# A selective-scan kernel on one core: loads of B, evacuation of the sums and the multiply of carried states placed later in the slot order

## The chip, the cores and the metric

The kernel runs on one core of a Trainium2 chip. The core has a tensor engine (PE, with PEld for its weight loads), a vector engine (DVE), a scalar engine (ACT), a general engine (POOL) and a sync engine (SP), each with its own instruction queue, and 16 DMA engines between HBM and on-chip memory. The metric is the device time of one execution in microseconds (us), median of several runs.

## The reference

The input is `x` of shape (8, 96, 128, 128), float32. Layer 0 adds to `x` a convolutional LSTM over the rows of a group-normalised `x`. Layer 1 adds to that a wavelet block: a wavelet transform of the group-normalised input, an attention factor on the three high bands, and on the low band (64 x 64 positions, so L = 4096) layer norm, a projection, a 3 x 3 convolution and a selective scan in four directions with 192 channels and 16 states. Then come a norm, a gate, a projection and the inverse wavelet transform. The scan is the part that the change touches:

```python
xs = jnp.concatenate([x_hwwh, jnp.flip(x_hwwh, -1)], axis=1)      # rows, columns, both reversed
x_dbl = jnp.einsum('bkdl,kcd->bkcl', xs, x_proj_w)
dts, Bs, Cs = jnp.split(x_dbl, [DT_RANK, DT_RANK + D_STATE], axis=2)
delta = jax.nn.softplus(...)                                       # from dts
def step(hst, inp):
    u_t, d_t, B_t, C_t = inp
    dA = jnp.exp(d_t[..., None] * A)
    hst = dA * hst + (d_t * u_t)[..., None] * B_t[:, :, None, :]
    y = jnp.einsum('bkdn,bkn->bkd', hst, C_t)
    return (hst, y)
_, ys = jax.lax.scan(step, h0, seq)
```

## The kernel before, in words

Layer 0 fills the first 3000 us or so. Then comes one long loop, `for s in range(total)` (L1140), of 3072 slots. A slot scans two states (GN = 2) over 512 positions (CH = 512) for 128 lanes, each lane a channel of one of two directions. Four slots (PASS = 4) are a pass over half of the states. A chunk of 512 positions takes 24 slots: two halves of the states, r = 0 and 1, and in each half three groups of lanes, q = 0, 1, 2. An image has 8 chunks in forward order (p = 0) and 8 in reverse (p = 1), and there are 8 images, so 128 chunks. `place(s)` (L908) gives chunk, r, q, the number of the block of B and C, and the first state. Slot numbers below are within the chunk, 0 to 23; a number over 23 is a slot of the next chunk.

What a slot does, engine by engine:

- ACT: `decay(s + 1)` (L1006) makes two exponentials, 128 x 512 each, into a PSUM tile `da`, of which there are two. At L1152 it copies the last column of the slot before as the carried state.
- POOL: `product(s + 3)` (L994) multiplies `du` by a tile `bt` of B for the slot three ahead (L1001), and adds the carried states to the border column (L1004).
- DVE: `scan(s)` (L1021) runs the recurrence at L1025, then in three slots of four L1191 multiplies by a tile `ct` of C. In the first slot of a pass (`by_pool`, L1014) POOL does that multiply one slot later (L1199).
- PE: `add_up` (L1027) transposes and adds the result into one PSUM tile `py` for the pass, which has a single buffer.
- SP: `load_bc(k, cols)` (L981) issues the load of block k of B (cols 0) or of C (cols 1), as two DMAs of 256 KB. There are five buffers of each. A block serves the same slot of the passes q = 0, 1 and 2; in the pass q = 2 it is used for the last time, and then block k + 5 goes into its buffer. B is loaded at the end of slot s for the block of slot s + 2 (L1202), and C for the block of slot s - 2 (L1204). So B is loaded in slots 6 to 9 and 18 to 21, C in slots 10 to 13 and 22 to 25. Three of four such blocks are first needed by slots 13, 14, 15 and 25, 26, 27 (the last three are slots 1, 2, 3 of the next chunk); the fourth is needed twelve slots later.

`evacuate` (L1088) runs in the first slot of each pass. ACT copies the finished `py` out of PSUM, into `half` when r = 0 (L1095), into `y` when r = 1 (L1102). For r = 1 it also enters a job: `y_store` (L1052), which stores y from ACT's DMA queue (p = 0), or `y_out` (L1056), which transposes it on PE, copies it on ACT and stores a part from ACT's queue at L1066 (p = 1).

All other work (wavelet analysis, projections, softplus, output, synthesis) is cut into jobs: generators that yield an engine, a cost, a number of half slots to wait since the job's last step, and resources that they take and give. `background` (L1132) is called once in the first slot of a pass and twice in the other three, and `now` counts these calls: they are the half slots. Each call gives every engine a budget (PE 1.1, ACT 0.9, DVE 0.7, POOL 1.3 us) and writes the job steps that fit. `border` (L956) is such a job: ACT makes the factor `ac` of the carried states (L965), then POOL multiplies it by them (L968) and sets a border column of `dl` (L969). `pin` (L453) fixes the order of the instructions on each engine as written.

Two rules of the built program matter too. SP and ACT issue their DMAs in order. All DMAs complete on eight semaphores, handed out in turn, and a DMA is not issued before the previous DMA of its semaphore has landed, whichever queue that one is on.

Of the kernel before, what the change touches and what calls it, by code (L numbers as in the profile page):

```python
# [56 lines left out]
def forward_kernel(ctx: ExitStack, tc: tile.TileContext, i, out):  # L57
# [29 lines left out]
    with ExitStack() as s:  # L87
# [15 lines left out]
        def place(lanes, chunk, src):  # L103
            for m in range(3):
                nc.sync.dma_start(wq[lanes, chunk, m, 0:96], src[:, m, :])
                nc.sync.dma_start(wq[lanes, chunk, m, 96:128], src[:, 3, 32 * m:32 * m + 32])
# [124 lines left out]
    with ExitStack() as s:  # L231
# [143 lines left out]
        for k in range(4):  # L375
            r, p, h0 = dtrow[k], k // 2, k % 2
# [76 lines left out]
        def pin():  # L453
            traced = tc.nc.cur_bb.bb.instructions
            for ins in traced[seen[0]:]:
                prev = pinned.get(ins.engine)
                if prev is not None:
                    tc.add_manual_dep(ins, prev.name, mybir.DependencyInfo(
                        mybir.DependencyClass.NoSync, mybir.DependencyReason.DATA), reason="order of the slots")
                pinned[ins.engine] = ins  # L460
            seen[0] = len(traced)
# [68 lines left out]
        BANK, SHORT, NONE = ("bank",), ("short",), ()  # L530

        def hasten(job):
            if not job.done and job.rank > -1e9:
                job.due, job.rank = min(job.due, now[0]), -1e9
                for a in job.after:
                    hasten(a)

        def drain(until):

            for job in until:  # L540
                hasten(job)
            jobs.sort(key=lambda j: j.rank)
            while not all(j.done for j in until):
                big = dict(SP=1e9, PE=1e9, ACT=1e9, DVE=1e9, POOL=1e9)
                write(dict(big), EARLY)
                write(dict(big), LATE)
                now[0] += 1
                pin()
# [351 lines left out]
        order = [(p, c) for p in range(2) for c in (range(NCHK) if p == 0 else reversed(range(NCHK)))]  # L900
        chunks = [(b, p, c) for b in range(B) for p, c in order]
        PASS = NS // GN // 2
        SLOTS = 6 * PASS
# [10 lines left out]
        def edges(ci):  # L914

            return (0, CH - 1) if chunks[ci][1] == 0 else (CH - 1, 0)

        def is_first(ci):
            return ci % NCHK == 0

        def is_last(ci):
            return ci % NCHK == NCHK - 1
# [33 lines left out]
        def border(ci, q):  # L956


            b, p, c = chunks[ci]
            e0 = edges(ci)[0]  # L960
            yield "ACT", 0.25, 1, NONE, NONE
            dl = inputs[ci, q][0]
            if not is_first(ci):
                ac = inputs[ci, q][2] = sp.tile([128, NS], F32, name="ac", bufs=6)
                nc.scalar.activation(ac, av[:, p, q, :], AF.Exp, scale=dl[:, e0:e0 + 1])  # L965
            yield "POOL", 0.4, 1, NONE, NONE
            if not is_first(ci):
                nc.gpsimd.tensor_mul(ac, ac, carries[b, p][:, q, :])  # L968
            nc.gpsimd.memset(dl[:, e0:e0 + 1], 1e30)  # L969
# [11 lines left out]
        def load_bc(k, cols):  # L981

            if k < NBLOCKS:
                (b, p, c), n0 = chunks[k // (2 * PASS)], GN * (k % (2 * PASS))
                if not all(j.done for j in analysed[b][0]):
                    drain(analysed[b][0])
                t = bcts[k, cols] = bcp.tile([128, GN, CH], F32, name="bt" if cols == 0 else "ct", bufs=5)
                n0 = 2 * n0 + GN * cols
                for h0 in range(2):
                    nc.sync.dma_start(t[64 * h0:64 * h0 + 64],  # L990
                                      bc_d[b][2 * p + h0, n0:n0 + GN, c * CH:c * CH + CH].unsqueeze(0)
                                      .to_broadcast([64, GN, CH]))
# [13 lines left out]
        def decay(s, j):  # L1006
            if s < total:
                ci, r, q, k, n0 = place(s)
                p = chunks[ci][1]
                if j == 0:  # L1010
                    das[s] = psh.tile([128, GN, CH], F32, name="da")
                nc.scalar.activation(das[s][:, j], inputs[ci, q][0], AF.Exp, scale=av[:, p, q, n0 + j:n0 + j + 1])  # L1012

        def by_pool(s):  # L1014
            return s % PASS == 0

        def halves(s):

            return 2 * s - (s + PASS - 1) // PASS
# [30 lines left out]
        stored, back, quarter, turns, flushed, ys = {}, {}, [], [], [], []  # L1050
# [81 lines left out]
        def background(**full):  # L1132

            for eng, us in full.items():
                left[eng] = us + min(left.get(eng, 0), 0)
            write(left, EARLY)
            write(left, LATE)
            now[0] += 1

        for s in range(total):  # L1140
            at_slot[0] = s
            ci, r, q, kb, n0 = place(s)
            b, p, c = chunks[ci]

            if by_pool(s - 3):
                add_up(s - 3)
            if not by_pool(s - 1):
                add_up(s - 1)

            if s and not by_pool(s - 1) and not is_last((s - 1) // SLOTS):  # L1150
                pc, _, pq, _, pn = place(s - 1)
                nc.scalar.copy(carries[chunks[pc][0], chunks[pc][1]][:, pq, pn:pn + GN], das[s - 1][:, :, edges(pc)[1]])  # L1152
            das.pop(s - 1, None)
            for j in range(GN):
                decay(s + 1, j)
            if s and s % PASS == 0:
                evacuate(s - 1)
            slot, step = s % SLOTS, ci % len(order)
            if slot == 0:
                if step == 0:  # L1160


                    if b > 0:
                        outs = output(b - 1, now[0] + 4, now[0] + 0.25 * IMAGE, turns)
                        synthesis(b - 1, now[0] + 0.2 * IMAGE, now[0] + 0.97 * IMAGE, [*outs, analysed[b - 1][1]])
                    turns = []
                    if b + 1 < B:
                        analysed[b + 1] = analysis(b + 1, now[0] + 4, now[0] + 0.71 * IMAGE)
                if is_first(ci):
                    carries[b, p] = sp.tile([128, 3, NS], F32, name="carry")  # L1170
                if ci + 1 < len(chunks):
                    after = analysed[b + 1][0] if step + 1 == len(order) else []
                    now0[0] = now[0] - halves(s)
                    dt_job[ci + 1] = add(now[0], load_dt(ci + 1), after, urgent=1000)
                    for t in range(3):
                        prepare(ci + 1, t, after)
                if p == 1:
                    back[ci] = [add(now[0] + 2 * (8 + PASS * t), forward_sum(ci, b, c, t), after=[stored[b, c, t]],
                                    take=("yf",), urgent=1000)
                                for t in range(3)]  # L1180
            if p == 1 and r == 1 and slot % PASS == 0 and not back[ci][q].done:
                drain([back[ci][q]])
            pool = by_pool(s)
            background(SP=1e9, PE=1.1, ACT=0.9, DVE=0.7, POOL=1.3)
            scan(s)
            product(s + 3)
            xb = xbs.pop(s)
            if not pool:
                background(SP=1e9, PE=1.1, ACT=0.9, DVE=0.7, POOL=1.3)
                hc = sums[s] = sp.tile([128, GN, CH], F32, name="hc")  # L1190
                nc.vector.tensor_mul(hc, das[s], bcts[kb, 1])  # L1191
            else:
                made = s, xb
            if by_pool(s - 1):
                sp1, xb = made
                pc, _, pq, pk, pn = place(sp1)
                if not is_last(pc):
                    nc.gpsimd.tensor_copy(carries[chunks[pc][0], chunks[pc][1]][:, pq, pn:pn + GN], xb[:, :, edges(pc)[1]])
                nc.gpsimd.tensor_mul(xb, xb, bcts[pk, 1])  # L1199
                sums[sp1] = xb  # L1200

            if place(s + 2)[2] == 2:  # L1202
                load_bc(place(s + 2)[3] + 5, 0)
            if s > 1 and place(s - 2)[2] == 2:  # L1204
                load_bc(place(s - 2)[3] + 5, 1)
            if r == 1 and slot % PASS == PASS - 1:
                free["dl"] += 1
            pin()
# [68 lines left out]
```

## Time and profile before

| | us |
|---|---|
| median of three runs | 15879.47 (15873.98 to 15884.72) |
| the profiled execution, its own time | 15881.9 |
| its span, first to last instruction | 15880.1 |
| stretch of the 3072 scans, first start to last end | 3567.9 to 15379.0, 11811.1 |
| busy in that stretch: DVE, POOL, PE, ACT | 10509.8, 10270.6, 8686.6, 7300.1 |
| DMA in that stretch | 0.72 of the 16 engines' time, 162 GB/s |

The page gives busy time by engine, then the span in 40 slices, DMA queues, groups of instructions (`out<-in`, count, busy us, mean ns, idle us of the engine before them and what ended it), and DMA issues. The view of waits gives who waited for whom: us in total, how many times, the longest. For SP a wait is time in which its queue stood still. Line numbers are those of the kernel before.

### The profile page before, as it was taken

How to read it: one execution, taken by the hardware profiler on the slowest of the kernel's cores; microseconds unless marked ns; L12 is line 12 of the kernel's file. 1: busy time of each engine (PE TensorE's matmuls, PEld its weight loads, DVE VectorE, ACT ScalarE, POOL GpSimd, SP SyncE). 2: the span in 40 equal slices, each digit the busy share in tenths (PEclk: the TensorE clock that was granted, in tenths of full speed). 3: DMA queues.
4: the chain of work that ended last, by engine and by line, in shares of the span. 5: the costliest groups of instructions: out<-in, count | busy, mean ns of one | idle time of the engine just before them, and what ended most of it. 6: DMA issues, size and time to landing. Idle time of an engine off the chain costs nothing. (4 is left out here: it accounts for less than half of the span.)

```text
span 15880.1 us, 146749 instructions
## 1 busy us (share of the span) xinstructions
PE 12017.8 (76%) x42850; PEld 6570.4 (41%) x42850; DVE 11728.4 (74%) x8612; ACT 8726.4 (55%) x15473; POOL 11270.4 (71%) x9544
## 2 busy tenths in 40 slices
PE   2999999586776777777777777777777777766666
PEld 0444444234444444444444444444444444444432
DVE  4333333209999988998899889888998898899871
ACT  0444444236766665666566656655665566555440
POOL 1333333009899987997798889878987898799760
PEclk9999999788887988888888888888888898877876
DMA  7333333246767777776777777777777777766653
GB/s 166 72 73 72 71 64 66 55 93 167 166 145 164 173 162 157 172 178 153 158 176 170 156 166 174 167 159 164 176 167 156 165 175 164 154 148 145 143 113 78
DMA packets 2458101, 2239.33 MB, mean 141 GB/s; under 512 B 1322929, under 2 KB 1523058, under 8 KB 2457043
## 3 DMA queue, kind: packets, MB, share of 16 engines
q1 hardware_dynamic: 1313491, 2007.56, 54.7%
q10 hardware_dynamic: 1143808, 222.38, 8.5%
q8 instruction: 344, 5.64, 0.2%
q14 instruction: 458, 3.75, 0.1%
HBM read 1862.20 MB, written 367.03 MB: 140 GB/s over the span
## 5 line engine op out<-in xcount | busy, mean ns | idle before, releaser
L1001 POOL TENSOR_TENSOR xb<-du,bt 128x1024 f32<-128x1024 f32 x3072 | 7245.7, 2362 | 330.9 <-DMA bt<-bc_d 169.6
L1025 DVE TENSOR_TENSOR_SCAN da<-da,xb 128x1024 f32<-128x1024 f32 x2304 | 5262.9, 2284 | 377.2 <-ACT da L1012 356.7
L1012 ACT ACTIVATE da<-dl,av 128x512 f32<-128x512 f32 x6144 | 4249.6, 692 | 1044.7 <-DVE hc L1191 494.7
L1039 PE MATMUL py<-ident,hc 128*128 128x128 f32 x18432 | 2882.3, 308 | 2400.6 <-DVE hc L1191 2272.9
L1039 PEld LDWEIGHTS py<-ident,hc 128*128 128x128 f32 x18432 | 2402.5, 159 | 3526.6 <-issue 1478.3
L1191 DVE TENSOR_TENSOR hc<-da,ct 128x1024 f32<-128x1024 f32 x2304 | 2813.2, 1221 | 552.5 <-DMA ct<-bc_d 390.9
L181 PE MATMUL pg<-hx,wq 128*128 128x512 f32 x4608 | 2019.7, 592 | 0.0
L1199 POOL TENSOR_TENSOR xb<-xb,ct 128x1024 f32<-128x1024 f32 x768 | 1809.3, 2356 | 99.3 <-DVE xb L1025 45.6
L1152 ACT COPY carry<-da 128x2 f32<-128x2 f32 x2016 | 319.9, 159 | 2721.8 <-DVE hc L1191 2492.7
L1025 DVE TENSOR_TENSOR_SCAN xb<-da,xb 128x1024 f32<-128x1024 f32 x768 | 1750.1, 2279 | 60.9 <-ACT da L1012 48.3
L584 PE MATMUL pd<-ph,wa 128*128 128x512 f32 x2304 | 1223.2, 663 | 262.7 <-ACT ph L578 142.3
L811 PE MATMUL pd<-ph,wg 128*128 128x504 f32 (+1 forms) x2304 | 1214.1, 659 | 204.5 <-DMA ph<-ll_d 124.4
L181 PEld LDWEIGHTS pg<-hx,wq 128*128 128x128 f32 x4608 | 871.7, 189 | 1106.7 <-issue 1106.3
L198 POOL TENSOR_TENSOR x1b<-xb,hx 96x512 f32<-96x512 f32 x256 | 302.7, 1183 | 1369.7 <-DVE hx L197 1124.4
L186 ACT ACTIVATE gate<-pg,gbias 32x512 f32<-32x512 f32 x768 | 523.3, 681 | 1185.2 <-PE pg L181 1185.2
L644 PE MATMUL pc<-xp,wc 97*128 97x512 f32 x2304 | 1143.6, 627 | 3.4 <-ACT bcs L674 3.4
L1039 PE MATMUL py<-ident,xb 128*128 128x128 f32 x6144 | 1006.5, 318 | 142.4 <-POOL xb L1199 140.5
L1039 PEld LDWEIGHTS py<-ident,xb 128*128 128x128 f32 x6144 | 879.2, 167 | 543.2 <-issue 266.7
L192 DVE TENSOR_TENSOR gate<-gate,gate 96x512 f32<-96x512 f32 x256 | 186.7, 729 | 840.9 <-ACT gate L186 840.9
L584 PEld LDWEIGHTS pd<-ph,wa 128*128 128x128 f32 x2304 | 452.7, 212 | 745.2 <-issue 439.9
L811 PEld LDWEIGHTS pd<-ph,wg 128*128 128x128 f32 x2304 | 461.7, 215 | 677.5 <-issue 580.3
L178 PE MATMUL pg<-x,wq 128*128 128x512 f32 x1536 | 703.4, 594 | 14.7 <-POOL x L168 14.7
(179 smaller groups left out, 12317.9 us busy)
## 6 DMA issues: line engine op xcount, KB each, us to landing
bt<-bc_d SPq DMA_DIRECT2D x2048, 256.0 KB
ct<-bc_d SPq DMA_DIRECT2D x2048, 256.0 KB
raw<-x_d SPq DMA_DIRECT2D x384, 288.0 KB
xb<-in_x SPq DMA_DIRECT2D x64, 1536.0 KB
du<-u_d SPq DMA_DIRECT2D x768, 128.0 KB
wa<-wa_d SPq DMA_DIRECT2D x192, 384.0 KB
xs<-in_x SPq DMA_DIRECT2D x64, 1024.0 KB
x_d<-x1b SPq DMA_DIRECT2D x792, 64.0 KB
```

Source lines behind the costliest of these rows:

```text
L178: nc.tensor.matmul(pg[m], wq[:, 3, m, :], xk[:, r, bs, 0:W], start=True, stop=False)
L181: nc.tensor.matmul(pg[m], wq[:, tap, m, :], hk[:, r, bs, tap:tap + W], start=False, stop=(tap == 2))
L186: nc.scalar.activation(gg[32 * m:32 * m + 32], pg[m][96:128], AF.Tanh, bias=gbias[96:128, m:m + 1])
L584: nc.tensor.matmul(pd, wa[:, 3 * ty + tx, :], ph[:, ty:ty + 8, tx:tx + W2], start=(ty == tx == 0), stop=(ty == 1 and tx == 2))
L644: nc.tensor.matmul(pc, wc[:, tap, d0:d0 + 128], xp[:, r + ty:r + ty + 8, tx:tx + W2], start=(tap == 0), stop=(tap == 8))
L811: nc.tensor.matmul(pd[:, :, c0:c1], wgs[g][:, 3 * ty + tx, :], ph[:, ty:ty + 8, c0 + tx - 1:c1 + tx - 1], start=(k == 0 and tx == 1), stop ...
L1001: nc.gpsimd.tensor_mul(xb, du.unsqueeze(1).to_broadcast([128, GN, CH]), bcts[k, 0])
L1012: nc.scalar.activation(das[s][:, j], inputs[ci, q][0], AF.Exp, scale=av[:, p, q, n0 + j:n0 + j + 1])
L1025: nc.vector.tensor_tensor_scan(h, da, xb, 0.0, ALU.mult, ALU.add)
L1039: nc.tensor.matmul(pys[key][:, 128 * t:128 * t + 128], hc[:, j, 128 * t:128 * t + 128], ident, is_transpose=True, skip_group_check=True, s ...
L1191: nc.vector.tensor_mul(hc, das[s], bcts[kb, 1])
L1199: nc.gpsimd.tensor_mul(xb, xb, bcts[pk, 1])
```

## The change

Three edits. The job `border` waits two half slots instead of one between ACT's factor and POOL's multiply. The load of B is written one slot later, in slots 7 to 10 and 19 to 22. The first call of `background` in a slot moves ahead of `evacuate`; the block that enters the jobs of the next chunk in slot 0 stays behind `evacuate`, so it too comes after that call. In the first slot of a pass that call is the only one.

```diff
-            yield "POOL", 0.4, 1, NONE, NONE
+            yield "POOL", 0.4, 2, NONE, NONE
...
             for j in range(GN):
                 decay(s + 1, j)
+            slot = s % SLOTS
+            if p == 1 and r == 1 and slot % PASS == 0 and not back[ci][q].done:
+                drain([back[ci][q]])
+            pool = by_pool(s)
+            background(SP=1e9, PE=1.1, ACT=0.9, DVE=0.7, POOL=1.3)
             if s and s % PASS == 0:
                 evacuate(s - 1)
-            slot, step = s % SLOTS, ci % len(order)
+            step = ci % len(order)
             if slot == 0:
...
-            if p == 1 and r == 1 and slot % PASS == 0 and not back[ci][q].done:
-                drain([back[ci][q]])
-            pool = by_pool(s)
-            background(SP=1e9, PE=1.1, ACT=0.9, DVE=0.7, POOL=1.3)
             scan(s)
             product(s + 3)
...
-            if place(s + 2)[2] == 2:
-                load_bc(place(s + 2)[3] + 5, 0)
+            if place(s + 1)[2] == 2:
+                load_bc(place(s + 1)[3] + 5, 0)
```

## The prediction

> **What bounds the kernel now.** I read the page first, then who waited for whom on DVE, SP, POOL and ACT, then the timeline around one long wait. From the page:
>
> ```profile
> PE 12017.8 (76%) x42850; PEld 6570.4 (41%) x42850; DVE 11728.4 (74%) x8612; ACT 8726.4 (55%) x15473; POOL 11270.4 (71%) x9544
> DVE  4333333209999988998899889888998898899871
> ...
> L1025 DVE TENSOR_TENSOR_SCAN da<-da,xb 128x1024 f32<-128x1024 f32 x2304 | 5262.9, 2284 | 377.2 <-ACT da L1012 356.7
> L1191 DVE TENSOR_TENSOR hc<-da,ct 128x1024 f32<-128x1024 f32 x2304 | 2813.2, 1221 | 552.5 <-DMA ct<-bc_d 390.9
> ```
>
> PE has the largest total, but that is an average over stages. The row of digits shows DVE at 8 and 9 tenths from the tenth slice on: in the stretch of the scans (11811.1 us) DVE is busy 10509.8, so it sets the pace, and only its 1301 idle us can be won. The last two lines name the two largest pieces: 390.9 us waiting for a C load, 356.7 for ACT's exponentials. The waits:
>
> ```profile
> DVE hc L1191 <- DMA ct<-bc_d: 390.9, 110, 12.9
> DVE da L1025 <- ACT da L1012: 356.7, 174, 8.8
> ```
>
> ```profile
> SPq L990 <- POOL xb L1004: 1040.7, 436, 17.0
> SPq L990 <- DMA y_d<-y: 283.3, 40, 10.7
> ```
>
> ```profile
> POOL ac L968 <- ACT ac L965: 443.1, 176, 13.5
> POOL xb L1001 <- DMA bt<-bc_d: 169.6, 57, 9.1
> POOL xb L1001 <- DVE da L1025: 133.0, 72, 6.9
> ```
>
> ```profile
> ACT y L1102 <- PE py L1039: 251.4, 159, 7.1
> ACT half L1095 <- PE py L1039: 200.2, 143, 4.9
> ```
>
> Each edit has its row: B loads standing for POOL (1040.7), evacuations standing for PE (251.4 + 200.2), POOL standing for the factor (443.1). None of these waits is DVE's own, so none counts in full. Why C loads come late is seen in the timeline:
>
> ```profile
> 7414.81 9.77 SPq L990 DMA_DIRECT2D ct<-bc_d  x4
> 7415.85 0.58 ACT L1102 COPY y<-py 128x512 f32<-128x512 f32 x1
> ...
> 7420.40 0.45 ACTq L1066 DMA_DIRECT2D y_d<-y  x1
> ...
> 7426.95 1.23 DVE L1191 TENSOR_TENSOR hc<-da,ct 128x1024 f32<-128x1024 f32 x1 [6.84 <-DMA ct<-bc_d]
> ```
>
> The four C loads are merged in one piece of 9.77 us, because SP stood still inside it: the second of them completes on the semaphore of a y store that ACT issues only at 7420.40, after evacuating y. DVE then waits 6.84 us.
>
> **The change part by part.** *B loads and the order of DMAs.* Same 2048 DMAs, same bytes. C loads stay where they are in SP's queue, behind the same B load: the block loaded in slot 21 before, and 22 after, waits for the same product on POOL. So SP's 1040.7 us is not what the C loads get back; what moves ahead of the B loads is one slot of job DMAs. What does change is which DMA shares a semaphore with which. I followed the wait lists of both built programs: for each C block first needed in slots 1, 2, 3, 13, 14, 15, the latest ACT slot that SP must have seen before it can issue the load. Before, 58 blocks (of the stretch's 762, some eight in each image) hang on an ACT store issued at most two slots ahead of the multiply, or in its slot. By the trace these 58 carry 242 us of DVE's 390.9: 54 for slot 1, 9 for slot 2, 100 for slot 3, 79 for slot 13. After, most of them hang on a store three to five slots ahead. I price each by blocks that had that distance before. Those 7 of slot 1 go to the rate 48.6/14 = 3.5 us, which gives 25 and saves 29; slot 2 saves 7; slot 3 saves 29 + 47 = 76; six blocks of slot 13 save 62. Against it: six of slot 13 come one slot nearer, 6 x 4 = +24; seven of slot 3 come to two slots, +15; and 14 of slot 1 hang on a y store that moves half a slot (2 us) later, +28. Sum: -174 + 67 = **-107**. From both sides: if all 242 went, -242; if the distances mean nothing, 0 or a loss (the rivals).
>
> The B loads lose time. DMA: Bandwidth & Descriptors, Rules for kernel authors, of the Trainium skill speaks against this edit: issue a DMA early, compute, and wait for it late. The row is POOL's 169.6 us for `bt`. I compared each B landing with POOL's first use of it: 155 of some 765 have under 4 us to spare, so loads 4 us later (a slot) make POOL wait 440 us more, and at 8 us 1457. By the rule alone I would book the 440. But products end at least 4.9 us ahead of their scan in 95 of 100 cases (median 6.7 to 13 us by slot), and taken one by one no scan would be held by 4 us; at 8 us, four for 1.7 us together. I take **+15** for what comes round through POOL's L1199 and L1004; bounds 0 and, should a quarter of 440 reach DVE, +110.
>
> *Evacuation.* 768 copies of 0.58 us stay. ACT's 452 us of waiting for PE shrinks only where the half slot holds ACT work to do first: by the built program in 231 of 767. At most 0.9 us (the budget) is won in each of 302 waits, 210 us in sum; times 231/767 gives 63 us of ACT time. ACT is 7300 of 11811 us busy, so this counts only where DVE then waits for `da`: 113 of its 411 us at scans had a waiting evacuation in the 8 us before, a quarter of 452. So 63/4, **-15**. Where PE is many us late, as for the 7.1, the next decay stays behind the copy and gains nothing. Queued behind the copy now are only the decay and what follows it; `py` is not written again before add_up in the pass's third slot. The y stores go out half a slot to a slot later, counted above. Bounds: +20 (a job step that stands still now stands ahead of the copy) and -60.
>
> *Next chunk's jobs* come one half slot later. They are due from slot 3 on at the earliest except the dt load; neither program has to finish a job by force between the first and last slot. 0, hidden by the slots left; if the cover were gone, one half slot (2 us) for each of 128 chunks, +256, which no row suggests.
>
> *Border.* 336 multiplies of 0.22 us and memsets of 0.10, moved past one half slot, some 2 us. POOL's 443.1 us would fall by about 300. DVE waits for POOL in this stretch 38 us in all, and POOL itself waits for the scan (133.0), so this is mostly slack: **-10**; bounds 0 and -40. The readers of `ac` and `dl` come eight slots later.
>
> Sum: -107 + 15 - 15 - 10 = -117. What is late next: ACT's `da`, DVE's second wait, since exponentials that had time while DVE stood still are now asked for sooner. I give back a quarter, and get **-90**. From the profiled execution's own 15881.9: 15792; the median of the runs is 2.4 lower: 15790.
>
> **The rivals.** (1) *Only the waiter changes.* The y stores still hold SP; they now hold B loads instead (in the built program one B block of slot 1 in each image then hangs on a store in the very slot of its product), and DVE loses about as much through POOL. Then only -15 - 10 + 15 and noise are left: 15870, within 0.2%. For it: the store waits stay in the program. Against it: the cover of the products.
>
> (2) *Slower, by crowding.* In slots 10 and 22 the last B block now stands directly ahead of the first C block, four DMAs in one slot. A block is 524 KB; at 162 GB/s and a share of 0.72 the engines would move 225 GB/s, so it needs 2.3 us (an estimate from those two numbers). 80 of 255 first C blocks have under 2.4 us to spare, and the sum of what they lack is 147 us. If SP is not standing still anyway, the C load is pushed by this much; without the gain from the store distances and with -10 from the rest: 15880 + 137 = 16017. It decides where the first C block of slots 13 and 25 lands under 2.3 us ahead of its multiply. Against it: where SP stands still and then issues everything in one burst, B was just ahead of C before too.
>
> (3) *More.* All 242 us go, ACT's own DMAs stand less for slow loads (tight ones fall from 155 to 128 in the built programs) and nothing is given back: -242 - 60 + 40 = -262, 15618.
>
> **How the numbers follow.** Forecast 0.50, its own range 15710 to 15850; more 0.11; only the waiter changes 0.18; slower 0.21. A measurement of this kernel tells 0.2%, 32 us, from no change. From the cases: faster 0.61, same 0.17, slower 0.22. The range takes in half of the third rival and the lower half of the slower one: 15650 to 15960.
>
> **What would show it.** Right: DVE's wait for `ct` falls from 391 to about 280, least in slot 13; the y stores stay among SP's waits; POOL's wait for `ac` falls to about 150 and that for `bt` grows by some hundreds without scans waiting for POOL (38 before, under 80); evacuation waits fall from 452 to about 390. Wrong: a `ct` wait that stays or grows in slots 1 and 13 (crowding), scans that wait for POOL by over 150 us (the cover is gone), or `da` waits that grow by as much as `ct` shrinks.

## The result, and the profile after

The changed kernel takes 15876.02 us (median of 12 runs, 15851.72 to 15886.64) against 15877.83 us (12 runs) for the kernel before: ratio 0.9998, 95% interval 0.9989 to 1.0007. That is no change within the 0.2% that can be told; predicted was 15790, a gain of 0.56%. The profiled execution has a span of 15876.5 us, and the stretch of the scans takes 11805.3 us instead of 11811.1. Line numbers from 1185 on are one higher than before.

The page's groups of the changed kernel, for the scan and for the multiply by C:

```profile
L1025 DVE TENSOR_TENSOR_SCAN da<-da,xb 128x1024 f32<-128x1024 f32 x2304 | 5264.6, 2285 | 353.8 <-ACT da L1012 324.2
L1192 DVE TENSOR_TENSOR hc<-da,ct 128x1024 f32<-128x1024 f32 x2304 | 2813.4, 1221 | 505.2 <-DMA ct<-bc_d 346.2
```

Next, the waits of the changed kernel: DVE's, then SP's, POOL's and ACT's (total us, times, longest).

```profile
DVE raw L817 <- PE pd L811: 489.2, 133, 17.0
DVE hc L1192 <- DMA ct<-bc_d: 346.2, 88, 13.4
DVE da L1025 <- ACT da L1012: 324.2, 175, 9.2
```

```profile
SPq L990 <- POOL xb L1004: 749.0, 323, 16.1
SPq L990 <- DMA y_d<-y: 216.7, 36, 10.0
```

```profile
POOL ac L968 <- ACT ac L965: 195.8, 74, 8.8
POOL xb L1001 <- DMA bt<-bc_d: 285.4, 85, 12.2
```

```profile
ACT y L1102 <- PE py L1039: 272.3, 139, 7.1
ACT half L1095 <- PE py L1039: 166.2, 124, 5.7
```

The waits that the edits aim at moved: SP stands 292 us less for POOL, POOL 247 us less for the factor. DVE's wait for C fell, but only by 45 us. The line that was not in the prediction is DVE's first: the synthesis' addition of matrix products to the raw rows (L817) waited 381.3 us before and waits 489.2 now. That alone is more than the wait for C gave back. In the stretch of the scans this wait goes from 167.4 to 273.9 (+106), C from 390.9 to 346.2 (-45), scans for ACT from 411.4 to 405.9; all long idle pieces of DVE together from 1140 to 1173 (+33), and DVE's own busy time from 10510 to 10472 (-38).

The traces split by the half slot in which DVE stood still (sums of its waits over 0.15 us in the stretch, in us) show where the C wait went. "Scans for ACT" takes in the carried states as well as the exponentials. The columns to the right are experiments told below.

| | before | changed | only B later | evacuation edit alone | changed, B as before | changed, C ahead of B |
|---|---|---|---|---|---|---|
| stretch of the scans | 11811.1 | 11805.3 | 11887.2 | 11786.9 | 11756.1 | 11841.2 |
| wait for C, slots 1 and 13 | 197.7 | 303.1 | 275.8 | 182.5 | 168.0 | 101.3 |
| wait for C, slots 2, 3, 14, 15 | 193.2 | 43.2 | 184.7 | 75.6 | 72.5 | 217.5 |
| raw rows for TensorE | 167.4 | 273.9 | 161.8 | 247.4 | 258.7 | 263.2 |
| scans for ACT | 411.4 | 405.9 | 389.7 | 477.8 | 459.8 | 450.2 |
| POOL for B | 168.6 | 284.4 | 308.1 | 157.5 | 179.6 | 294.2 |

So the C wait nearly vanished in slots 2, 3, 14 and 15 (193 to 43), and grew by 105 us in slots 1 and 13, the first C blocks of each half.

The same waits can be split by cause. For each C block that DVE waited for, the trace tells when SP issued the second of its two DMAs, and what SP had last stood for before it (stands of over 0.7 us). A block is *held by a store* if that issue came after DVE was ready and SP had stood for the landing of a store of ACT. It *landed late* if the issue came in time. A few blocks were issued late for other reasons (43 us before, 6 after).

| us | before | changed | only B later | evacuation edit alone | changed, B as before | changed, C ahead of B |
|---|---|---|---|---|---|---|
| held by a store, all slots | 138.9 | 83.4 | 152.5 | 49.1 | 50.9 | 96.8 |
| landed late, slots 1 and 13 | 81.3 | 219.6 | 136.1 | 173.0 | 158.8 | 94.9 |
| landed late, other slots | 127.7 | 37.4 | 137.8 | 26.5 | 15.4 | 114.1 |

Both causes are in the changed kernel. Blocks held by a store fell by 56 us, and late landing in slots 1 and 13 grew by 138. Of this growth 92 us come with the evacuation edit alone, where B has not moved: SP then stands for a store ahead of the B blocks, and issues them and the first C block in one burst. Bursts with four or more DMAs of B ahead of the C block cost 20 us in these slots before, 121 with the evacuation edit alone and 139 in the changed kernel.

### The profile page after: what moved, and what is told of

Same layout as the page of the kernel before. It is cut to its first block, busy times and chain, and to the rows that moved or that the text cites. A ratio compares the mean times of both kernels' runs of the same rounds, so it can differ in the third digit from the quotient of the medians.

```text
span 15876.5 us, 146579 instructions
## 1 busy us (share of the span) xinstructions
PE 11948.0 (75%) x42850; PEld 6560.5 (41%) x42850; DVE 11690.9 (74%) x8612; ACT 8721.7 (55%) x15473; POOL 11278.9 (71%) x9544
## 5 line engine op out<-in xcount | busy, mean ns | idle before, releaser
L1192 DVE TENSOR_TENSOR hc<-da,ct 128x1024 f32<-128x1024 f32 x2304 | 2813.4, 1221 | 505.2 <-DMA ct<-bc_d 346.2
L1025 DVE TENSOR_TENSOR_SCAN xb<-da,xb 128x1024 f32<-128x1024 f32 x768 | 1750.1, 2279 | 81.3 <-ACT da L1012 52.3
L811 PE MATMUL pd<-ph,wg 128*128 128x504 f32 (+1 forms) x2304 | 1247.7, 677 | 118.5 <-DMA ph<-ll_d 98.9
```

The costliest lines, as they stand in the source:

```text
L811: nc.tensor.matmul(pd[:, :, c0:c1], wgs[g][:, 3 * ty + tx, :], ph[:, ty:ty + 8, c0 + tx - 1:c1 + tx - 1], start=(k == 0 and tx == 1), stop ...
L1025: nc.vector.tensor_tensor_scan(h, da, xb, 0.0, ALU.mult, ALU.add)
```

## Experiments

**One edit at a time.** The first two runs are B alone and the border alone.

```diff
-            if place(s + 2)[2] == 2:
-                load_bc(place(s + 2)[3] + 5, 0)
+            if place(s + 1)[2] == 2:
+                load_bc(place(s + 1)[3] + 5, 0)
```

> The load of B a slot later alone; evacuation and border as before. Theory A (a gain that was given back): the gain of the whole change, DVE's 45 us less for C loads, came from new neighbours in the order of DMAs, and was eaten by DVE's wait for PE in the synthesis jobs (L817, 167 to 274 us in the stretch of the scans), which comes from jobs moved by half a slot. The jobs are not moved here, so that wait stays at 150 to 190 us. In this built program as many C blocks as before (54 a run of some 56 chunks' pairs) hang on a store at most two slots ahead, so DVE's wait for C stays at 370 to 410 us and the time within 0.2% of before (15850 to 15910). Theory B (slack: none of the edits touches DVE): the same time, but POOL's wait for B rises by 100 us or more with no scan that waits longer for POOL. Crowding (the slower rival of the prediction): DVE's wait for C in slots 1 and 13 grows by 50 us or more and the kernel is 0.3% or more slower.

Measured: ratio 1.0051 (1.0037 to 1.0064), +81 us. DVE's waits of this kernel:

```profile
DVE hc L1191 <- DMA ct<-bc_d: 460.4, 107, 12.9
```

The wait for C is 70 us longer, and that lies in slots 1 and 13 (198 to 276), where the last B block now stands directly ahead of the first C block. POOL waits 139 us more for B, and scans wait for POOL 58 us instead of 22. Of these 78 us, 55 are blocks that landed late and 23 are blocks that a store held longer. The crowding is real, at rather more than a third of the 147 us of the second rival.

```diff
-            yield "POOL", 0.4, 1, NONE, NONE
+            yield "POOL", 0.4, 2, NONE, NONE
```

> The multiply of the carried states one half slot later, alone. Both theories: POOL's wait for the factor falls from 443 to about 200 us, DVE's idle time stays within 20 us, and the time within 0.2% of before (15850 to 15910). If POOL is what sets the pace after all, 0.5% or more faster.

Measured: ratio 0.9965 (0.9953 to 0.9978), -52 us. POOL's wait for the factor falls from 443 to 133 us. What DVE gets of it is spread thin: 40 us less idle (1140 to 1100), 17 of them at C, 16 at a sum that POOL makes for the output job. On its own it beats both kernels.

**The evacuation edit in halves.** First the background call ahead of the evacuation, with the next chunk's jobs entered at the same count of half slots as before:

```diff
...
+            background(SP=1e9, PE=1.1, ACT=0.9, DVE=0.7, POOL=1.3)
             if s and s % PASS == 0:
                 evacuate(s - 1)
...
+            now[0] -= 1
...
-            background(SP=1e9, PE=1.1, ACT=0.9, DVE=0.7, POOL=1.3)
+            now[0] += 1
```

> The first background call ahead of the evacuation, with the due times of the jobs entered in slot 0 set back by the half slot that they would gain; B loads and border as before. Theory A: the jobs keep their phase, so DVE's wait for PE at L817 stays below 200 us; ACT's wait for PE at evacuations falls by some 60 us and DVE's for ACT by about 15; the time is 0 to 0.3% faster (15830 to 15890). Theory B: within 0.2%. If the y stores that go out later are what took the gain back, DVE's wait for C grows by 30 us or more and the kernel is slower by 0.2% or more.

Measured: 1.0035 (1.0023 to 1.0048), +55 us: outside what was expected. The raw rows wait 210 us in the stretch, 42 more than before and not below 200, though the jobs of the next chunk keep their due times. Then the other half: the evacuation stays ahead, and only the next chunk's jobs come behind that call.

```diff
             if s and s % PASS == 0:
                 evacuate(s - 1)
...
+            background(SP=1e9, PE=1.1, ACT=0.9, DVE=0.7, POOL=1.3)
...
-            background(SP=1e9, PE=1.1, ACT=0.9, DVE=0.7, POOL=1.3)
```

> The jobs of the next chunk entered one half slot later (the block of slot 0 behind the first background call), with the evacuation, the B loads and the border as before. Theory A: this alone brings the loss, DVE's wait for PE at L817 goes from 167 to 230 us or more in the stretch of the scans, and the kernel is 0.3 to 0.8% slower (15925 to 16005). Theory B: within 0.2% (15850 to 15910), L817 under 200 us.

Measured: 1.0135 (1.0122 to 1.0149), +222 us. The prediction had booked this at zero. The raw rows wait 191 us, not the 230 or more that was expected, so it is not they that make the loss. Scans wait 555 us for ACT instead of 411, 161 of them in slot 22 (53 before), and the wait for C is 63 us longer. The four single effects add up to +306 us, yet together they measured -2, so the two halves don't add. My reading was that each half shifts one set of jobs against the other, while the whole edit shifts both and keeps their order. The whole edit alone tests what this says of the time (here against the changed kernel):

```diff
-            yield "POOL", 0.4, 2, NONE, NONE
+            yield "POOL", 0.4, 1, NONE, NONE
...
-            if place(s + 1)[2] == 2:
-                load_bc(place(s + 1)[3] + 5, 0)
+            if place(s + 2)[2] == 2:
+                load_bc(place(s + 2)[3] + 5, 0)
```

> The whole evacuation edit alone (first background, drain and pool ahead of the slot-0 block and of the evacuation, so that both the jobs that the evacuation enters and the next chunk's jobs come one half slot later), with the B loads and the border as before. Phase theory (evacuation alone +55 and next-chunk jobs alone +222 us are prices of shifting one set of jobs against the other; shifted together they keep their order): changed kernel -2, less B's +81 and border's -52, is -31: 15,840 us, ratio 0.998 (0.9965 to 1.001). Additive theory: +55 +222 = about 16,150 us, ratio 1.017. In either case the wait for C in slots 2, 3 and 14 is small (the tight blocks fall), and in slots 1 and 13 it stays near 200 us, as B is not moved.

Measured: 0.9978 (0.9970 to 0.9985), 32 us less than the median before; the additive theory is out by 1.9%. Its DVE waits:

```profile
DVE raw L817 <- PE pd L811: 461.3, 120, 16.1
DVE da L1025 <- ACT da L1012: 406.9, 171, 11.7
DVE hc L1192 <- DMA ct<-bc_d: 258.1, 70, 9.8
```

Here the C gain stands alone: 391 to 258, -133 us. Slots 2 and 3 alone fall by 147, and slot 14 rises by 30. Of it only 24 us reach the stretch, because the raw rows' wait has grown by 80 and the scans' wait for ACT by 66.

**B in company.** The changed kernel with only the B edit taken back:

```diff
-            if place(s + 1)[2] == 2:
-                load_bc(place(s + 1)[3] + 5, 0)
+            if place(s + 2)[2] == 2:
+                load_bc(place(s + 2)[3] + 5, 0)
```

> The changed kernel with the B loads put back where they were (evacuation edit and border stay). Crowding theory (B loaded a slot later sits directly ahead of the first C block and delays it): the scans' wait for C in slots 1 and 13 goes from 303 to about 200 us, the time to about 15,790 us, ratio 0.9945 (0.992 to 0.998). Rival (the loss comes from the waits of the raw rows for TensorE, 274 us, not from B): ratio 0.999 to 1.001, the C wait in slots 1 and 13 stays near 300. Additive theory of the parts: about 16,090 us, ratio 1.014.

Measured: 0.9969 (0.9958 to 0.9980), less than hoped. The C wait in slots 1 and 13 falls to 168 as expected, but scans wait 54 us more for ACT than in the changed kernel. Set against the changed kernel's 0.9998, moving B costs 0.29% in company, about 46 us; set against the evacuation edit alone, the border adds 0.09%, which the intervals don't tell from nothing.

If the order of the two blocks at the end of a half slot were the cause, writing C first should cure it:

```diff
-            if place(s + 1)[2] == 2:
-                load_bc(place(s + 1)[3] + 5, 0)
             if s > 1 and place(s - 2)[2] == 2:
                 load_bc(place(s - 2)[3] + 5, 1)
+            if place(s + 1)[2] == 2:
+                load_bc(place(s + 1)[3] + 5, 0)
```

> The changed kernel with the C load written ahead of the B load at the end of a half slot, so that the last B block of a chunk no longer stands directly ahead of the first C block in the issuing queue. Crowding theory: the scans' wait for C in slots 1 and 13 falls from 303 to about 200 us and the time by 60 to 100 us: 15,790 us, ratio 0.994 (0.992 to 0.997). Rival (crowding is not between these two blocks but of the queue as a whole, or the B wait takes its place): ratio 0.999 to 1.002, the wait moves to B (285 us to over 350) or stays.

Measured: 1.0020 (1.0013 to 1.0027). This expectation fell for the time. The first table's last column shows why: slots 1 and 13 drop from 303 to 101, but slots 2, 3, 14 and 15 rise from 43 to 218. A part of this is crowding that moves on: the last B block now stands ahead of the second C block instead of the first, and late landing falls by 125 us in slots 1 and 13 and rises by 77 in the others. Another part is no crowding at all. In the changed kernel, once in each of six images, the second DMA of the C block for slot 13 has the semaphore of a store of `u` that ACT has just issued:

```profile
6261.06 1.23 SPq L990 DMA_DIRECT2D bt<-bc_d  x2
6262.39 16.86 SPq L990 DMA_DIRECT2D ct<-bc_d  x7
6262.97 0.56 ACTq L695 DMA_DIRECT2D u_d<-turn_u  x1
6278.81 1.23 DVE L1192 TENSOR_TENSOR hc<-da,ct 128x1024 f32<-128x1024 f32 x1 [12.77 <-DMA ct<-bc_d]
```

The store takes 11 us to land, SP stands inside the piece of C loads for as long, and the six multiplies of slot 13 wait 74 us. With C written ahead of B the same store holds the B block, and behind it the C block for slot 14, for 68 us:

```profile
6266.15 13.02 SPq L990 DMA_DIRECT2D bt<-bc_d  x2
6267.68 0.56 ACTq L695 DMA_DIRECT2D u_d<-turn_u  x1
```

With B as before it holds slot 14 too, for 51 us. So a new order of two loads also deals anew which load shares a semaphore with which store, and this run cannot tell crowding from that by its time alone.

**The raw rows.** The first addition of the synthesis yields one half slot behind its products; I gave it two:

```diff
-                    yield "DVE", 0.68, (1 if px == 0 else 0), NONE, (BANK + ("ph",) if px else NONE)
+                    yield "DVE", 0.68, (2 if px == 0 else 0), NONE, (BANK + ("ph",) if px else NONE)
```

> The changed kernel with the first addition of the synthesis two half slots behind its matrix products instead of one. If the 106 us that the raw rows' wait for TensorE has grown are what ate the gain of the C loads: that wait falls from 274 to below 100 us and the time by 100 to 170 us: 15,740 us, ratio 0.9915 (0.989 to 0.995). Rival (the work on TensorE is late as a whole and the wait comes back elsewhere, or later jobs take longer to finish): ratio 0.998 to 1.003 with the wait of the raw rows small and another, of scans for ACT or C, grown by as much.

Measured: 0.9926 (0.9914 to 0.9939), 0.72% under the changed kernel. Its DVE waits:

```profile
DVE hc L1192 <- DMA ct<-bc_d: 408.7, 101, 15.7
...
DVE raw L817 <- PE pd L811: 240.5, 56, 16.4
```

In the stretch the raw rows' wait falls from 274 to 26, and 62 us come back as waits for C and 82 as scans waiting for ACT. The C blocks held by a store cost 174 us here, 83 in the changed kernel. The control is the same edit on the kernel before:

> Control for the run with the synthesis addition two half slots behind its products: the same edit on the kernel before. There the raw rows wait 167 us for TensorE in the stretch of the scans, against 274 in the changed kernel. If that grown wait is what ate the gain of the change: this edit is worth less here, about 107 x 167/274 = 65 us, 15,810 us, ratio 0.996 (0.994 to 0.998). Rival (the edit is a gain of its own, which has nothing to do with the change): the same 0.7 to 0.75% as on the changed kernel, ratio 0.9925 or lower.

Measured: 1.0010 (1.0003 to 1.0016): not even the 0.4% that I had expected, rather a small loss.

```profile
DVE hc L1191 <- DMA ct<-bc_d: 389.8, 105, 14.1
...
DVE raw L817 <- PE pd L811: 330.1, 63, 15.6
```

There the wait falls only from 167 to 117 in the stretch. Two more runs cross this edit with the others. The evacuation edit and the border, B as before, with the longer wait:

> The changed kernel without the B edit (evacuation edit and border stay) and with the synthesis addition two half slots behind. If the two causes (B moved: +0.29% in company of the rest; raw rows' wait: 0.72%) are separate, they add: ratio 0.9897, 15,720 us (0.988 to 0.992), with the C wait near 240 us and the raw rows' wait near 26. If they are two names for the same slack: ratio 0.992 to 0.995.

Measured: 0.9901 (0.9888 to 0.9915), 15706.49 us: the fastest of all versions, ahead of both kernels. The ratio is the sum that two separate causes would give, but one number goes against that expectation:

```profile
DVE hc L1192 <- DMA ct<-bc_d: 384.0, 72, 15.2
DVE da L1025 <- ACT da L1012: 356.4, 173, 10.3
DVE raw L817 <- PE pd L811: 237.2, 48, 15.9
```

The C wait is back at 384, not 240. The trace tells what brought it back: 185 us of it are blocks held by a store of ACT, against 51 without the longer wait. In six images a block of slot 3 stands for a store of `turn_y` (88 us), and twelve blocks of slot 2 stand for stores of y (82 us); in the kernel without the longer wait none of these places is held. The gain of this kernel lies in the raw rows (167 before to 24 in the stretch) and in DVE's busy time (-44). The same without the evacuation edit:

> The kernel before with only the border edit and the synthesis addition two half slots behind; evacuation and B as before. If the evacuation edit's gain (C wait in slots 2, 3 and 14 gone) is real once the raw rows' wait is out of its way, this is slower than the same with the evacuation edit by the 130 us of C wait less what else comes: ratio 0.992 (0.990 to 0.995) against 0.990. Rival (the evacuation edit gives nothing): ratio 0.990 or lower here.

Measured: 0.9962 (0.9950 to 0.9975), outside the expected 0.990 to 0.995, and the same as the border alone. So, all with the border edit, there is a square: neither 0.9965, longer wait alone 0.9962, evacuation edit alone 0.9969, both 0.9901. Neither of the two gains anything next to the border without the other; together they gain 0.6%. That is not the gain at C set free, as the expectation had it. From the longer wait alone to both, the wait for C goes from 377 to 384, the raw rows' wait from 119 to 24, scans for ACT from 382 to 468, all long idle pieces of DVE together from 1058 to 1011 and its busy time by -25; the stretch is 79 us shorter. So in the pair the longer wait takes the raw rows' wait away, which it does only beside the evacuation edit (without it 117 to 119 us stay), while late stores take the gain at C back. Why the longer wait needs the evacuation edit is not shown.

**What makes the raw rows late.** The trace shows one place where the growth is largest and repeats: at slot 21 of an image's thirteenth chunk this wait was 0.2 to 1.2 us in six images before, and is 6.7 to 8.0 us after. The timeline of the kernel before at that place (start, us, engine, line; in brackets the idle before):

```profile
6111.08 1.73 ACTq L679 DMA_DIRECT2D dt_d<-bcs  x1
...
6114.27 0.58 ACT L1102 COPY y<-py 128x512 f32<-128x512 f32 x1
...
6115.40 1.86 PE L811 MATMUL pd<-ph,wg 128*128 128x504 f32 x4
...
6117.29 0.68 DVE L817 TENSOR_TENSOR raw<-raw,pd 64x512 f32<-64x512 f32 x1 [0.57 <-PE pd L811]
```

And of the changed kernel:

```profile
6108.21 5.41 ACTq L679 DMA_DIRECT2D dt_d<-bcs  x1
...
6113.67 0.59 ACT L1102 COPY y<-py 128x512 f32<-128x512 f32 x1 [6.85 <-DMA bc_d<-bcs]
...
6114.31 0.99 PE L1061 MATMUL pt<-ident,y 128*128 128x128 f32 x4 [4.40 <-ACT y L1102]
...
6115.09 3.25 PE L811 MATMUL pd<-ph,wg 128*128 128x504 f32 x4
...
6118.38 0.68 DVE L817 TENSOR_TENSOR raw<-raw,pd 64x512 f32<-64x512 f32 x1 [7.85 <-PE pd L811]
```

Read downward, this is a chain through three engines. The background call, now first, writes a job's stores directly ahead of the evacuation; issuing one of them keeps ACT's queue for 5.41 us. The copy of y waits behind it and the stores just ahead of it 6.85 us, PE's transposes of y wait for the copy, and the synthesis' products stand behind the transposes in PE's order. They are also slow: four take 3.25 us instead of 1.86. These are the two stretches of the changed kernel (busy us of PE, PEld, DVE, ACT and POOL; then the granted clock, the DMA engines' share and GB/s):

```profile
6109.90:6114.30 4.40, 0.01 (x1) 0.00 (x0) 0.63 (x1) 0.63 (x2) 0.00 (x0) 1.00 1.07 170
6114.30:6118.40 4.10, 4.09 (x11) 2.25 (x12) 0.02 (x1) 2.09 (x5) 2.52 (x3) 0.58 1.07 105
```

After PE had idled 4.4 us, the granted clock is 0.58; in the kernel before it was 1.00 there. TensorE: Matmul & The Clock Gate of the Trainium skill (Part 1: The HAM clock gate) says that the clock goes to half after some 3.4 us of idleness, which fits these rows. Over the stretch these 2016 products take 1356 us instead of 1315, so slower products are at most 41 of the 106 us.

In total ACT's copy of y idles 41.8 us behind those stores, and its factors `ac` 31.9; before, both were 0. I tried to move the stores away, one half slot behind the copy that fills their tile:

```diff
-                yield "ACT", 1.0, 0, NONE, NONE
+                yield "ACT", 1.0, 1, NONE, NONE
                 for dst, src in ((bc_d[b][odr], bcs[bp.start:bp.start + 32]),
```

> The changed kernel with the three stores of a projected block (B, C, dt; issued by ACT, up to 5.8 us of ACT's queue in one issue) one half slot behind the copy that fills their tile, instead of in the same half slot. Theory (these issues now stand directly ahead of ACT's copy of the sums, which idles 42 us behind them and 32 us ahead of the decay factors, where before it was 0 and 0; the raw rows' wait follows): that idle falls to under 20 us, the raw rows' wait from 274 to about 220, the time by 40 to 70 us, ratio 0.9965 (0.994 to 0.999). Rival (the issues stand ahead of some other ACT step wherever they are put): ratio 0.999 to 1.004, the idle behind them as large, ahead of the scans' factors instead.

Measured: 1.0136 (1.0121 to 1.0152). The idle at these two places fell to 6 and 19 us, and came back ahead of the carried states; ACT's waits:

```profile
ACT carry L1152 <- issue: 188.4, 38, 14.8
ACT carry L1152 <- DMA bc_d<-bcs: 58.1, 17, 7.2
```

In the changed kernel these were 119.1 and 16.9. The raw rows wait 354 us here. The rival was right, and by far more than it said. So the chain is shown in the trace for one place of each of six images, some 40 of the 106 us (44.4 against 4.0). For the other 66 the cause stays open, and it is another one: of the 274 us, 230 passed while TensorE worked with no idle piece over 0.3 us (154 of 167 before). There the products were under way, and DVE came to the addition too soon behind them; which of the shifted jobs brought that about was not followed.

## Why the prediction was wrong, point by point

Two steps of the sum failed. The term for the C loads, -107, had no place for what the same edits do to the first C blocks of each half, and came out at -45. And the sum had no term at all for DVE's wait for the raw rows, which grew by 106 us; the quarter given back was booked at another wait.

- **C loads, -107: failed in the sum.** The mechanism, late stores on a shared semaphore, is in the traces: blocks held so cost 139 us before and 83 after. But with the blocks that landed late in a burst behind such a stand, ACT's stores account for 257 us of the wait before (the prediction had 242) and for 289 after: their hold did not go, it moved. With B unmoved the whole wait fell by 133; slot 13 fell by 41 (priced -38), slots 2 and 3 by 147 (priced -68), and slots 1 and 14 rose by 26 and 30 (slot 1 priced -1). With B moved, slots 1 and 13 came out at +105 instead of -39. Two prices were wrong there. Crowding stood outside the sum, as a rival that excludes this gain, because "B was just ahead of C before too"; in fact both happen, and bursts with four or more DMAs of B ahead of C cost 139 us in these slots instead of 20. And six blocks of slot 13 were held by a store anew, for 74 us (16 before), where the sum had +24 for six that come one slot nearer.
- **B loads, +15 with bounds 0 to +110: mis-sized and misplaced.** +81 us alone, +46 in company. The rule for early issue that the prediction quotes was right in sign. POOL's wait for B grew by 116 us in the changed kernel, not by 440, and the scans' wait for POOL was 22 us before and 26 after. As predicted, the cover of the products held; the price was paid by the C loads behind.
- **Evacuation, -15: failed.** ACT's waits for PE fell from 452 to 438, not to 390, and ACT stood 74 us behind issues of stores at two places where it had not stood before. The bound of +20 named exactly this, "a job step that stands still now stands ahead of the copy", but looked for the price at ACT; it appeared at DVE's raw rows, at +80 (edit alone) to +106, some 40 of them by way of PE as shown.
- **Next chunk's jobs, 0: wrong reason.** Alone they cost 222 us. By the run of the whole edit alone (-32) that matters little for the full change, where the y jobs are shifted with them. A late due time is no cover when a step's place among other steps moves.
- **Border, -10 with bounds 0 to -40:** -52 alone, outside the bounds; 0.09% in company, no more than noise. Of the 310 us that POOL waited less, most was slack, as said.
- **A quarter given back to ACT's `da`: wrong address.** Scans for ACT went from 411 to 406 in the full change. What came next was the raw rows' wait for TensorE's `pd`, 381.3 us before (167.4 of them in the stretch): it stood between the two DVE waits that the prediction showed, and had no place in its sum. It grew by 106, and the longer wait behind the products, which takes it away, is worth 0.72% of the changed kernel's time.
- **"Only its 1301 idle us can be won": not quite.** DVE's busy time fell by 38 us, mostly in one line (last section).

Against the measured stretch: C -45, raw rows +106, scans for ACT -6, all other idle -22, busy -38, together -5. The first rival ended at the measured time by luck. Its first half is seen, stores that hold SP with B blocks behind them, but DVE lost nothing to POOL; it lost to the C loads behind those blocks, and to the raw rows.

## What to carry to other kernels

When an edit moves one set of loads towards another on the same queue, put the crowding into the sum beside the gain instead of into a rival, and see which transfers are ahead of the tight one for several slots, not only next to it. Where two queues share a few completion semaphores, an edit that moves any DMA can deal anew which load stands for which store: work the pairs out for the new program, and price a held block by what held blocks cost (here 6 to 15 us each). In a kernel whose engines run a fixed order, list every wait of the bounding engine before forecasting, also those that the edit doesn't name: here a shift of some jobs by half a slot cost up to 1.4%, the parts of one edit didn't add, and a saved wait is kept only if the next consumer down the order has room (here one more half slot for one addition, worth 0.7% with the evacuation edit and nothing without).

## What the hardware showed unexpectedly

Issuing a DMA can hold an engine for longer than its arithmetic: 5.41 us above, beside a copy of 0.59. The store of `dt` from ACT took 0.62 us to issue in the median (4.5 to landing) and up to 5.83 in the changed kernel; 78 of ACT's issues took over 2 us, 61 before. DMA: Bandwidth & Descriptors of the Trainium skill (Issuing engines are not separate DMA queues) calls this time usually small relative to the DMA; the median agrees, the tail doesn't. Around the issue of 5.41 us the DMA engines' share was 1.00 (6104.0 to 6118.4), so a full set of DMA engines may be what holds it. But it was 0.89 during the issue itself, and 1.04 during the issue of 1.73 us in the kernel before; no run tested it.

A DVE instruction with two inputs in SBUF varied more than fourfold, here in the kernel before (min, median, max in ns):

```profile
L851 DVE SCALAR_TENSOR_TENSOR ysum<-uo,dsum,ysum x128: 720/1234/3346, 5004.9 to 15609.6; 128x512 f32<-128x512 f32 x64, 64x512 f32<-64x512 f32 x64
```

Those over 1.5 us overlapped POOL's work for 97% of their time, those up to 1.0 us for 49%. SBUF — State Buffer of the Trainium skill (SBUF: two separate sides) describes a port pair that such an instruction and POOL lock against each other. By where this line fell, it cost 200 us before and 170 after, most of the 38 us that DVE's busy time shrank.
